# Scatter DMAs of a graph layer on GpSimd: a wait on TensorE's work two blocks on is taken out

## The chip, the cores and the metric

The kernel runs on one core of one Trainium2 chip. The metric is the device time of one launch in microseconds (us), from the start to the end of the program on that core; lower is better. PE is TensorE, DVE is VectorE, ACT is ScalarE, POOL is GpSimd and SP is SyncE. A "DMA" here is a transfer that one of these engines issues and that the core's 16 DMA engines carry out.

## The reference

One message-passing layer on a graph with 6250 nodes of 64 features and 206250 edges of 64 features, followed by a residual and a layer norm:

```python
row, col = edge_index                      # src, dst
msg = concat([x[col], edge_attr], axis=1)  # 206250 x 128
h = relu(msg @ W1a.T + b1a)
h = h @ W1b.T + b1b
agg = segment_sum(h, row, 6250) / maximum(counts, 1)[:, None]
z = relu(concat([x, agg], axis=1) @ W2a.T + b2a) @ W2b.T + b2b
out = concat([z, x], axis=1) @ Wr.T + br
return layernorm(x + out)
```

The work is in `relu(msg @ W1a.T + b1a)` for every edge and in the sum of these rows over the edges of a node. The edges come sorted by `dst`, so a run of edges needs few different rows of `x` for `col`; their `src` is in no order, so the rows have to be brought together by node before they are summed.

## The kernel before, in words

**Blocks.** The edges are cut into 124 blocks of 13 tiles of 128 edges. For each block the kernel computes the first layer's rows (`relu(...)`, 128 numbers, a count of 1 and the low bits of the node, 130 floats in all) into one of four SBUF buffers `orow0` to `orow3`, block k into buffer k % 4, and writes them to slots in DRAM that are grouped by node (128 nodes to a bin, 49 bins). Later, groups of slots are read back (`read`, L1457, tile `rt`) and summed by node: DVE builds a 0/1 matrix of slot against node (L1486, tile `oh`), PE multiplies it with the rows (L1505), and DVE adds the result to `part` (L1565).

**Two kinds of row.** In blocks 4 to 103 some of the edges are "joined": PE first sums up to four edges of the same node (L1267 and L1280, with the matrix `marks` of L1235, L1240 and L1241), and one row of the sum is kept, in a row of four that is called a quad. A block has two such joins of 3 tiles each, and nine of the blocks (9, 11, ... 25) have three. So a block has 13 tiles of single rows outside blocks 4 to 103, 7 with two joins, and 4 with three; to these come 2 or 3 joins.

**Scatters.** Each tile of single rows, and each join, is written to DRAM by one indirect DMA that POOL issues, with 128 slots that DVE has computed (`rowidx`, L1204, and `qidx`, L1167): L1395 for single rows and L1366 for quads. There are 985 of the one and 209 of the other, 1194 in all: 13 for a block with no join, 9 with two joins, 7 with three.

**Order.** PE, ACT, DVE and SP run in the order of the program text, which is written out by hand. Iteration k of the main loop has, in this order, the number of each edge's slot for block k + 1, the rows of block k, the sums that are due, and `scatter(k - LEAD)` with `LEAD = 2`. POOL's scatters are not in this fixed order: they are placed by the scheduler of the framework by when it reckons that their inputs are there. On the chip POOL then takes them strictly in the order that was placed, and one that waits holds up all behind it.

**Who waits for a scatter.** `low_bits(k)` (L1346, on ACT) is the first to write to block k's buffer, and waits until all scatters of block k - 4 have landed; the evictions from PSUM to the buffer follow it on ACT (L1358 for single rows, L1283 for quads). Reads (L1457, on SP) wait for the scatters whose rows they may hold, and the last group of reads for all of them. After the last scatter come only these last sums and the second layer of the nodes that are summed. The lines that matter:

```python
def low_bits(k):                                            # ACT, L1346
    ...
    nc.scalar.copy(orow_of(k, j0, BLK - j0)[:, :, H + 1], lo[:, k * BLK + j0 : (k + 1) * BLK])

def hidden(k, parts):                                       # PE L1355, ACT L1358
    ...
        done[k, c] = nc.tensor.matmul(ps[:, j, :], rhs[:WIDE, ...], m[:WIDE, :H], ...).ins.name
    nc.scalar.activation(orow_of(k, k0, n)[:, :, :H], ps[:, :n, :], AF.Relu)

def join_rows(k, i):                                        # PE L1280, ACT L1283
    ...
    done[k, f"join{i}"] = nc.tensor.matmul(ps[:, j, :], rj[:, ...], m, ...).ins.name
    nc.scalar.activation(mrow[:, g0 : g0 + 2, :], ps, AF.Relu)
```

The dictionary `done` keeps the names of PE's instructions: the matmul of tile c of block k, the last of its i-th join, and the last matmul of the first sum of iteration k (`"first"`) and of its rest (`"rest"`, both L1505).

Of the kernel before, what the change touches and what calls it, by code (L numbers as in the profile page):

```python
# [469 lines left out]
LEAD = 2  # L470
JOIN, QUAD, MARKS = 3, 4, 3
# [15 lines left out]
def fast_path(  # L487
# [42 lines left out]
    NGR = NT // NG  # L530
# [3 lines left out]
    BLK = NG  # L534
# [17 lines left out]
    def joined(k):  # L552
        if not JOIN_FROM <= k < JOIN_TO:
            return 0
        return 3 if k in THRICE else 2
# [194 lines left out]
    with (  # L750
# [16 lines left out]
        def orow_of(k, j, n=1):  # L767

            c = ROOM - BLK + j
            return orows[k % ROWS][:, c : c + n, :]  # L770

        def mrow_of(k, i):
            return orows[k % ROWS][:, i * QUAD : (i + 1) * QUAD, :]
# [252 lines left out]
        def bins_of(k):  # L1026


            ep_ = epoch_of[k]
            c0, j0 = k * BLK, JOIN * joined(k)  # L1030
            oh = ohs.pop(k)
            if joined(k) != joined(k - 1):
                starts_at(joined(k))
            t = direct(k) + 1
            had = slp.tile([P, 2 * HALF * t], BF16, name="had", padded_shape=[P, 2 * HALF * T])
            by_bin = oh.rearrange("p (b t) -> p b t", t=t)
            if j0:
                g = joined(k)
                joh = johs[k] = slp.tile([P, JOIN, g, NQB], BF16, name="joh", padded_shape=[P, JOIN, JOINS, NQB])
                nc.vector.tensor_tensor(  # L1040
                    joh,
                    ramp[:, None, None, :NQB].to_broadcast([P, JOIN, g, NQB]),
                    hi[:, c0 : c0 + j0].rearrange("p (j t) -> p t j", t=JOIN)[:, :, :, None].to_broadcast([P, JOIN, g, NQB]),
                    op=ALU.is_equal,
                )
            nc.vector.tensor_tensor(
                by_bin[:, :, 1:],
                ramp[:, : 2 * HALF, None].to_broadcast([P, 2 * HALF, BLK - j0]),
                hi[:, None, c0 + j0 : c0 + BLK].to_broadcast([P, 2 * HALF, BLK - j0]),
                op=ALU.is_equal,  # L1050
            )
            nc.vector.tensor_tensor_scan(had, on[:, : 2 * HALF * t], oh, 0.0, op0=ALU.mult, op1=ALU.add)  # L1052
            oh, had = (v.rearrange("p (b t) -> p b t", t=t) for v in (oh, had))
            hads[k] = had
            return oh, had
# [282 lines left out]
        done = {}  # L1338
# [21 lines left out]
        def scatter(k):  # L1360
            ep_ = epoch_of[k]
            e = epochs.index(ep_)
            j0 = JOIN * joined(k)
            for i in range(joined(k)):
                q = join_at[k] + i
                s = nc.gpsimd.indirect_dma_start(  # L1366
                    out=qep.rows.rearrange("(q r) f -> q (r f)", r=QUAD),
                    out_offset=bass.IndirectOffsetOnAxis(ap=qidx[:, q : q + 1], axis=0),
                    in_=mrow_of(k, i).rearrange("p r f -> p (r f)"),
                    in_offset=None,  # L1370
                )
                tc.declare_no_dep(s.ins, group="qslots", reason="each slot is written once")
                tc.add_to_no_dep_group("qslots", s.ins)
                tc.add_to_no_dep_group(f"qblock{k}", s.ins)
                scattered["q", k, i] = s.ins.name
                if k < EARLY:
                    tc.declare_no_dep(s.ins, group="qcleared", reason="no edge has these slots yet")
                if k == EARLY and i == 0:
                    for c in qcleared:
                        tc.add_manual_dep(  # L1380
                            s.ins, c.name,
                            mybir.DependencyInfo(mybir.DependencyClass.Sync, mybir.DependencyReason.DATA),
                            reason="edges may have these slots",
                        )
                for j, st in enumerate(qep.steps[:-1]):
                    if st.at <= k:
                        tc.declare_no_dep(s.ins, group=f"qreads{j}", reason="later edges have later slots")
            pace = (
                {9: BLK - 1, 10: "join0", 11: "join1", 12: "join2"} if j0 == 3 * JOIN
                else {6: 9, 8: BLK - 1, 10: "join0", 12: "join1"} if j0 == 2 * JOIN  # L1390
                else {j0: 9, j0 + 2: "first", 7: BLK - 1, 9: "join0", 11: "rest"}
            )
            for j in range(j0, BLK):
                t = k * BLK + j
                s = nc.gpsimd.indirect_dma_start(  # L1395
                    out=ep_.rows,
                    out_offset=bass.IndirectOffsetOnAxis(
                        ap=rowidx[:, k % RING * BLK + j : k % RING * BLK + j + 1], axis=0
                    ),
                    in_=orow_of(k, j)[:, 0, :],  # L1400
                    in_offset=None,
                )
                tc.declare_no_dep(s.ins, group=f"slots{e}", reason="each slot is written once")
                tc.add_to_no_dep_group(f"slots{e}", s.ins)
                tc.add_to_no_dep_group(f"block{k}", s.ins)
                scattered[t] = s.ins.name
                later = (min(k + LEAD, NGR - 1), pace.get(j))
                if later in done:
                    tc.add_manual_dep(
                        s.ins, done[later],  # L1410
                        mybir.DependencyInfo(mybir.DependencyClass.Sync, mybir.DependencyReason.DATA),
                        reason="first-layer rows are kept ahead of the scatters",
                    )
                for i, st in enumerate(ep_.steps[:-1]):
                    if st.at <= k:
                        tc.declare_no_dep(s.ins, group=f"reads{i}", reason="later edges have later slots")
                if k < EARLY:
                    tc.declare_no_dep(s.ins, group="cleared", reason="no edge has these slots yet")
                if k == EARLY and j == 0:
                    for c in cleared:  # L1420
                        tc.add_manual_dep(
                            s.ins, c.name,
                            mybir.DependencyInfo(mybir.DependencyClass.Sync, mybir.DependencyReason.DATA),
                            reason="edges may have these slots",
                        )
# [261 lines left out]
        for k, ep_ in enumerate(epoch_of):  # L1687
# [7 lines left out]
            j0 = JOIN * joined(k)  # L1695
# [7 lines left out]
            if k == 0:  # L1703
# [5 lines left out]
                ahead = bins_of(1)  # L1709
# [30 lines left out]
            if k + 2 < NGR:  # L1740
                columns(k + 2)
                ahead = bins_of(k + 2)
# [74 lines left out]
            if k >= LEAD:  # L1817
                scatter(k - LEAD)
# [15 lines left out]
        for k in range(NGR - LEAD, NGR):  # L1834
            scatter(k)
# [188 lines left out]
```

## Time and profile before

| | |
|---|---|
| three runs, median (lowest to highest) | 1638.09 us (1637.46 to 1638.39) |
| the profiled execution's own time | 1640.12 us |
| its span, first to last instruction | 1638.2 us |
| PE, DVE, ACT, POOL busy | 88%, 83%, 67%, 71% of the span |
| mean granted clock of PE | 0.96 |
| DMA | 393.44 MB, 240 GB/s over the span |

The profiled execution is 0.12% above the median of the three runs, and 1.9 us of its time lie outside the span. In the rows of the profile, `x985` is a count of instructions, the two numbers behind it are their busy time in us and the mean of one in ns, and what stands behind the second bar is the idle time of the engine just before them with what ended it. "issue" means that the engine waited for nothing that the profile shows. In a timeline a row has the start in us, the duration in us, the engine, the line and the operation, and in brackets the idle time before it and its releaser.

### The profile page before, as it was taken

What the parts mean: (1) busy time and instruction counts of PE and PEld (TensorE: products, weight loads), DVE (VectorE), ACT (ScalarE), POOL (GpSimd) and SP (SyncE); (2) the same over time, 40 slices, a digit from 0 to 9 for tenths busy, and PEclk for the clock granted to TensorE, in tenths of its full rate; (3) what the DMA queues carried; (4) which work ended last, traced back from release to release, by engine and by line L of the source; (5) the groups of instructions that cost most, each with busy time, mean ns of one, the idle gap of its engine ahead of it and who ended that gap; (6) DMA issues with size and microseconds to landing.
All of it is one profiled execution on the core that took longest, in us unless ns stands there. A gap on an engine that the chain in (4) does not pass through costs nothing.

```text
span 1638.2 us, 33212 instructions
## 1 busy us (share of the span) xinstructions
PE 1436.9 (88%) x10881; PEld 1306.3 (80%) x10881; DVE 1359.4 (83%) x3176; ACT 1102.8 (67%) x2247; POOL 1160.3 (71%) x1250
## 2 busy tenths in 40 slices
PE   6688888989999999999999999999986998799587
PEld 5577777778888888888888888888876998798476
DVE  7598888887888888999999999999966886776476
ACT  3289999987877777778878788877852344332044
POOL 6777777777777777777777777777776777777700
PEclk9699999999999999999999999999988999999788
DMA  8768888887887988677677667676879999897472
GB/s 208 218 227 288 289 285 293 293 262 240 251 259 227 269 237 246 203 231 216 202 222 217 216 204 235 199 227 194 237 229 342 324 324 290 265 280 241 132 207 78
DMA packets 230179, 393.44 MB, mean 240 GB/s; under 512 B 43205, under 2 KB 164935, under 8 KB 229743
## 3 DMA queue, kind: packets, MB, share of 16 engines
q1 hardware_dynamic: 155629, 224.57, 48.4%
q0 software_dynamic: 48240, 121.28, 21.0%
q10 hardware_dynamic: 26130, 45.38, 7.9%
q8 instruction: 89, 1.46, 0.4%
q14 instruction: 91, 0.75, 0.1%
HBM read 217.82 MB, written 173.25 MB: 239 GB/s over the span
## 4 chain that ended last, share of the span: by engine, by line
PE 55%; ACT 15%; DMA 14%; DVE 8%; issue 4%; POOL 2%; ACTq 1%; SPq 0%; DVEq 0%; POOLq 0%
PE h_ps L1505 23%; PE h_ps L1267 11%; DMA rows<-orow,rowidx 9%; PE h_ps L1355 9%; PE h_ps L1280 5%; ACT rhs L1320 4%; ACT rj L1272 3%; ACT orow L1283 2%; POOL rows L1395 2%; DMA rt<-rows 2%; DVE marks L1235 1%; ACT orow L1358 1%; ACT marks L1240 1%; ACT rhs L1318 1%; PE cnt_ps L1094 1%
## 5 line engine op out<-in xcount | busy, mean ns | idle before, releaser
L1395 POOL DMA_INDIRECT rows<-orow,rowidx x985 | 952.6, 967 | 329.8 <-issue 174.1
L1505 PE MATMUL h_ps<-rt,oh 128*128 128x129 f32 x4036 | 504.0, 280 | 43.8 <-DVE oh L1486 39.4
L1505 PEld LDWEIGHTS h_ps<-rt,oh 128*128 128x128 f32 x4036 | 479.3, 195 | 46.5 <-issue 40.8
L1486 DVE TENSOR_TENSOR oh<-ramp,rt 128x768 f32<-128x768 bf16 (+2 forms) x427 | 317.8, 779 | 46.0 <-DMA rt<-rows 42.3
L1267 PE MATMUL h_ps<-marks,side 128*128 128x512 f32 x1254 | 317.3, 402 | 2.8 <-ACT xr_now L1655 2.2
L1355 PE MATMUL h_ps<-mv,rhs 124*128 124x128 f32 x1970 | 278.3, 287 | 31.6 <-ACT orow L1358 31.5
L1280 PE MATMUL h_ps<-mv,rj 128*128 128x130 f32 x1672 | 234.1, 286 | 72.4 <-ACT orow L1283 45.5
L1280 PEld LDWEIGHTS h_ps<-mv,rj 128*128 128x128 f32 x1672 | 212.8, 193 | 106.2 <-ACT orow L1283 57.6
L1355 PEld LDWEIGHTS h_ps<-mv,rhs 124*128 124x128 f32 x1970 | 249.6, 198 | 35.8 <-ACT orow L1358 33.4
L1267 PEld LDWEIGHTS h_ps<-marks,side 128*128 128x128 f32 x1254 | 229.7, 190 | 48.3 <-ACT xr_now L1655 3.5
L1235 DVE TENSOR_TENSOR marks<-quad_ramp,ramp 128x1024 fp32r<-128x1024 f32 x209 | 250.6, 1203 | 0.0
L1366 POOL DMA_INDIRECT quads<-orow,qidx x209 | 202.3, 968 | 66.1 <-issue 18.4
L1358 ACT ACTIVATE orow<-h_ps 128x384 f32<-128x384 f32 (+1 forms) x287 | 151.4, 536 | 143.5 <-PE h_ps L1355 138.0
L1272 ACT COPY rj<-h_ps 128x512 f32<-128x512 f32 x209 | 119.7, 588 | 77.4 <-PE h_ps L1267 76.8
L1565 DVE TENSOR_TENSOR part<-part,h_ps 128x387 f32<-128x387 f32 (+2 forms) x232 | 113.1, 488 | 68.4 <-PE h_ps L1505 67.6
L1241 ACT ACTIVATE marks<-marks,ones 128x512 fp32r<-128x512 f32 x209 | 150.9, 722 | 6.8
L1283 ACT ACTIVATE orow<-h_ps 128x260 f32<-128x260 f32 x418 | 139.8, 389 | 23.3 <-PE h_ps L1280 19.4
L1240 ACT ACTIVATE marks<-quad_ramp,z_act 128x512 fp32r<-128x512 f32 x209 | 149.4, 715 | 0.0
L1052 DVE TENSOR_TENSOR_SCAN had<-ramp,bins 128x400 bf16<-128x400 bf16 (+1 forms) x124 | 135.0, 1089 | 17.1 <-ACT bins L1073 4.5
L1318 ACT ACTIVATE rhs<-rhs,from_win 60x896 f32<-60x896 bf16 (+1 forms) x116 | 130.5, 1125 | 2.9
L1320 ACT ACTIVATE rhs<-rhs,ones 60x896 f32<-60x896 f32 (+1 forms) x116 | 130.2, 1122 | 2.9
L1346 ACT CAST orow<-lo 128x7 f32<-128x7 bf16 (+1 forms) x124 | 24.2, 195 | 150.9 <-DMA rows<-orow,rowidx 139.1
(189 smaller groups left out, 1471.9 us busy)
## 6 DMA issues: line engine op xcount, KB each, us to landing
rt<-rows SPq DMA_DIRECT2D x145, 390.0 KB
rt<-quads SPq DMA_DIRECT2D x98, 390.0 KB
rhs<-in_edgeT SPq DMA_DIRECT2D x91, 224.0 KB
rt<-rows SPq DMA_DIRECT2D x98, 195.0 KB
enat<-in_edgeJ SPq DMA_DIRECT2D x91, 192.0 KB
rows<-orow,rowidx POOLq DMA_INDIRECT x985
rows<-padrow ACTq DMA_DIRECT2D x12, 1300.0 KB
quads<-padrow ACTq DMA_DIRECT2D x11, 1300.0 KB
```

Source lines behind the costliest of these rows:

```text
L1235: nc.vector.tensor_tensor(m[:, :n, :], all_q[:, None, :].to_broadcast([P, n, QUAD * P]), z[:, :n, None].to_broadcast([P, n, QUAD * P]), op ...
L1267: nc.tensor.matmul(ps, s[:, p, i * JOIN + t, :], m[:, t, :], start=t + p == 0, stop=t == JOIN - 1 and p == 1,)
L1272: nc.scalar.copy(rj, ps)
L1280: done[k, f"join{i}"] = nc.tensor.matmul(ps[:, j, :], rj[:, (g0 + j) * P : (g0 + j + 1) * P], m, start=True, stop=True).ins.name
L1283: nc.scalar.activation(mrow[:, g0 : g0 + 2, :], ps, AF.Relu)
L1320: nc.scalar.activation(rhs[D:WIDE, :], rhs[D:WIDE, :], AF.Relu, bias=ones[D:WIDE, :1], scale=-1.0)
L1355: done[k, c] = nc.tensor.matmul(ps[:, j, :], rhs[:WIDE, of * P : (of + 1) * P], m[:WIDE, :H], start=True, stop=True).ins.name
L1358: nc.scalar.activation(orow_of(k, k0, n)[:, :, :H], ps[:, :n, :], AF.Relu)
L1366: s = nc.gpsimd.indirect_dma_start(out=qep.rows.rearrange("(q r) f -> q (r f)", r=QUAD), out_offset=bass.IndirectOffsetOnAxis(ap=qidx[:, q ...
L1395: s = nc.gpsimd.indirect_dma_start(out=ep_.rows, out_offset=bass.IndirectOffsetOnAxis(ap=rowidx[:, k % RING * BLK + j : k % RING * BLK + j ...
L1486: nc.vector.tensor_tensor(res[:, at_tile : at_tile + nb * n, :], ramp[:, None, :].to_broadcast([P, nb * n, P]), node[:, :, None].to_broadc ...
L1505: m = nc.tensor.matmul(of_bin(b), oh[:, at_tile, :], rt[:, j * n + t, : H + 1], start=t0 + t == st.lo[b], stop=t0 + t == st.hi[b] - 1,)
```

## The change

In `scatter(k)`, the table `pace` and the dependency made from it are taken out. The table gave some of the single-row scatters of block k one more thing to wait for: a given piece of PE's work on block k + 2, such as the matmul of tile 9 or tile 12 or the last matmul of a join. Without it a scatter waits for its rows (ACT), for its slot numbers (DVE), and for the scatter eight places ahead of it to have landed, as all scatters did before and do now.

```diff
             def scatter(k):
                 ...
-            pace = (
-                {9: BLK - 1, 10: "join0", 11: "join1", 12: "join2"} if j0 == 3 * JOIN
-                else {6: 9, 8: BLK - 1, 10: "join0", 12: "join1"} if j0 == 2 * JOIN
-                else {j0: 9, j0 + 2: "first", 7: BLK - 1, 9: "join0", 11: "rest"}
-            )
             for j in range(j0, BLK):
                 t = k * BLK + j
                 s = nc.gpsimd.indirect_dma_start(
                 ...
                 scattered[t] = s.ins.name
-                later = (min(k + LEAD, NGR - 1), pace.get(j))
-                if later in done:
-                    tc.add_manual_dep(
-                        s.ins, done[later],
-                        mybir.DependencyInfo(mybir.DependencyClass.Sync, mybir.DependencyReason.DATA),
-                        reason="first-layer rows are kept ahead of the scatters",
-                    )
```

The instructions of PE, DVE, ACT and SP keep their order. On POOL the number and the kind of the instructions stay as they are, and their order changes. The first place is POOL where block 59 begins (buffers: 56 in `orow0`, 57 in `orow1`, 58 in `orow2`, 59 in `orow3`). In brackets stands what a scatter waits for: a DMASW number is the scatter eight places ahead of it. Before:

```order
L1366 DMA quads_66<-orow2_141,qidx_222 54976x520 [waits DMASW6_49,DVE_49,Activation_49]
L1395 DMA rows0_64<-orow0_139,rowidx_103 125440x130 [waits DMASW7_49,PE_49]
L1366 DMA quads_66<-orow2_141,qidx_222 54976x520 [waits DMASW0_49,Activation_49]
L1395 DMA rows0_64<-orow1_140,rowidx_103 125440x130 [waits DMASW1_49,PE_49]
L1395 DMA rows0_64<-orow3_142,rowidx_103 125440x130 [waits DMASW2_49,DVE_49,Activation_49]
L1395 DMA rows0_64<-orow3_142,rowidx_103 125440x130 [waits DMASW3_49]
L1395 DMA rows0_64<-orow1_140,rowidx_103 125440x130 [waits DMASW4_49,PE_49]
L1395 DMA rows0_64<-orow3_142,rowidx_103 125440x130 [waits DMASW5_49,Activation_49]
L1395 DMA rows0_64<-orow1_140,rowidx_103 125440x130 [waits DMASW6_49,PE_49]
```

The fifth row is block 59's first scatter. Ahead of it stand 522 scatters; three of block 57's and four of block 58's, all with a wait on PE, come after it, between those of blocks 59 and 60. The same place now:

```order
L1390 DMA rows0_64<-orow2_141,rowidx_103 125440x130 [waits DMASW6_49]
L1366 DMA quads_66<-orow2_141,qidx_222 54976x520 [waits DMASW7_49,DVE_49,Activation_49]
L1366 DMA quads_66<-orow2_141,qidx_222 54976x520 [waits DMASW0_49,Activation_49]
L1390 DMA rows0_64<-orow3_142,rowidx_103 125440x130 [waits DMASW1_49,DVE_49,Activation_49]
L1390 DMA rows0_64<-orow3_142,rowidx_103 125440x130 [waits DMASW2_49]
L1390 DMA rows0_64<-orow3_142,rowidx_103 125440x130 [waits DMASW3_49]
```

Each block's scatters stand together, in the order of the blocks: 529 of them, all of blocks 0 to 58, are ahead of block 59's first, and none waits for PE. L1390 is the former L1395; the change takes out lines above it.

The second place is POOL where block 107 begins (13 tiles to a block, no joins; 104 is in `orow0`, 105 in `orow1`, 106 in `orow2`, 107 in `orow3`). Before:

```order
L1395 DMA rows0_64<-orow0_139,rowidx_103 125440x130 x3
L1395 DMA rows0_64<-orow2_141,rowidx_103 125440x130 x5
L1395 DMA rows0_64<-orow3_142,rowidx_103 125440x130 x2
L1395 DMA rows0_64<-orow1_140,rowidx_103 125440x130
L1395 DMA rows0_64<-orow3_142,rowidx_103 125440x130 x2
L1395 DMA rows0_64<-orow1_140,rowidx_103 125440x130 x3
L1395 DMA rows0_64<-orow3_142,rowidx_103 125440x130 x6
```

And now:

```order
L1366 DMA quads_66<-orow3_142,qidx_222 54976x520 x2
L1390 DMA rows0_64<-orow0_139,rowidx_103 125440x130 x13
L1390 DMA rows0_64<-orow1_140,rowidx_103 125440x130 x13
L1390 DMA rows0_64<-orow2_141,rowidx_103 125440x130 x13
L1390 DMA rows0_64<-orow3_142,rowidx_103 125440x130 x13
```

Before, four tiles of block 105 and four of block 106 are left over when block 107 begins (the third row of before); now none is.

## The prediction

> **What bounds the kernel now.** I read the page's busy times first, then the idle time ahead of POOL's scatters, then the timelines. By busy time POOL looks idle for three tenths of the span.
>
> ```profile
> PE 1436.9 (88%) x10881; PEld 1306.3 (80%) x10881; DVE 1359.4 (83%) x3176; ACT 1102.8 (67%) x2247; POOL 1160.3 (71%) x1250
> L1395 POOL DMA_INDIRECT rows<-orow,rowidx x985 | 952.6, 967 | 329.8 <-issue 174.1
> L1366 POOL DMA_INDIRECT quads<-orow,qidx x209 | 202.3, 968 | 66.1 <-issue 18.4
> ```
>
> The waits, grouped (us in total, times, longest):
>
> ```profile
> POOL rows L1395 <- issue: 174.1, 571, 0.3
> ACT orow L1346 <- DMA rows<-orow,rowidx: 139.1, 23, 13.7
> ```
>
> 571 of POOL's gaps end without any wait, and each is 174.1 / 571 = 0.305 us. So a scatter costs POOL 0.967 + 0.305 = 1.272 us even when nothing holds it. 1194 of them take 1193 x 0.305 + 952.6 + 202.3 = 1518.8 us.
>
> ```profile
> 14.15 1.13 POOL L1395 DMA_INDIRECT rows<-orow,rowidx  x1 [8.04 <-ACT orow L1358]
> 1555.99 0.95 POOL L1395 DMA_INDIRECT rows<-orow,rowidx  x1 [0.30 <-issue]
> ```
>
> The first scatter starts at 14.15 and the last ends at 1556.94, 1542.8 us later. POOL is therefore held up for only 1542.8 - 1518.8 = 24.0 us in the whole run (the same from the groups: 329.8 + 66.1 - 8.04 ahead of the first - 363.9 = 24.0). From 14 to 1557 us POOL is the limit or close to it. Other engines stand ahead of it: ACT's 139.1 us is `low_bits` waiting for scatters of four blocks earlier to free a buffer. The stages (busy us and count by engine, granted clock, DMA share, GB/s):
>
> ```profile
> 340.00:699.20 359.20, 331.82 (x2518) 299.94 (x2516) 308.01 (x745) 284.04 (x571) 265.21 (x276) 1.00 0.80 241
> 1267.80:1380.00 112.20, 112.20 (x995) 110.77 (x994) 98.12 (x175) 46.47 (x62) 85.03 (x89) 1.00 1.02 320
> 1557.00:1638.20 81.20, 63.38 (x477) 57.36 (x477) 57.50 (x160) 38.74 (x182) 0.00 (x0) 0.88 0.50 143
> ```
>
> Between 340 and 699 PE is busy for 92%, and POOL issues 276 scatters, which at 1.272 us would take 351 of the 359 us: here PE's chain sets the pace, POOL waits a little. After the last scatter there are 81.3 us of last sums. PE's view of that seam:
>
> ```profile
> 1562.99 6.22 PE L1505 MATMUL h_ps<-rt,oh 128*128 128x129 f32 x36 [26.68 <-DVE oh L1486]
> ```
>
> PE has nothing to do for 26.68 us and then starts 6 us after the last scatter's end. So the end of the run is the end of POOL's scatters plus 81.3 us.
>
> **The change, part by part.** *Removed:* the wait on PE. What it costs is seen where a scatter with that wait has a gap over 0.3 us, as in these two:
>
> ```profile
> 651.97 0.96 POOL L1395 DMA_INDIRECT rows<-orow,rowidx  x1 [1.11 <-PE h_ps L1355]
> 658.96 0.95 POOL L1395 DMA_INDIRECT rows<-orow,rowidx  x1 [0.97 <-PE h_ps L1280]
> 626.48 0.60 ACT L1358 ACTIVATE orow<-h_ps 128x512 f32<-128x512 f32 x1
> 630.04 0.49 ACT L1358 ACTIVATE orow<-h_ps 128x384 f32<-128x384 f32 x1
> ```
>
> By the order these scatters are tiles 9 and 11 of block 53; ACT's two rows are the evictions that made their rows, 25 and 28 us earlier. They wait for block 55's PE work, and lose 1.11 - 0.305 = 0.8 and 0.7 us of POOL. All such losses lie within the 24.0 us. That is the ceiling of any gain on POOL, unless a scatter itself gets cheaper.
>
> *Moved:* each block's three or four held-back scatters go two blocks earlier, to their own block. The gain is how far POOL is ahead at the last moment when it must wait for rows. I take block 59's first rows, near the end of the stretch that PE paces:
>
> ```profile
> 698.62 0.60 ACT L1358 ACTIVATE orow<-h_ps 128x512 f32<-128x512 f32 x1 [1.95 <-PE h_ps L1355]
> 0.00:699.20 699.20, 391.78 (x402) 0.96 0.81 253
> 0.00:699.20 699.20, 114.93 (x119) 0.96 0.81 253
> 0.00:699.20 699.20, 11.37 (x60) 0.96 0.81 253
> ```
>
> The last three rows are the counts up to 699.2 us of L1395, of L1366 and of ACT's L1346. The 60th `low_bits` is block 59's, and its rows are there at 698.62 + 0.60 = 699.22. By then POOL had issued 402 + 119 = 521. In the new order all of blocks 0 to 58 can be out: 529. Can POOL have done them? 14.15 + 529 x 1.272 = 687.0, 12 us before the rows of block 59 come, so yes, if the earlier rows come when they came before; POOL then waits out these 12 us in small gaps. That they do I take from PE, DVE and ACT having the same instructions in the same order, and waiting for no scatter yet at that time: in the timeline ACT's first waits for a buffer are these two:
>
> ```profile
> 329.93 0.20 ACT L1346 CAST orow<-lo 128x7 f32<-128x7 bf16 x1 [1.10 <-DMA quads<-orow,qidx]
> 1034.77 0.20 ACT L1346 CAST orow<-lo 128x7 f32<-128x7 bf16 x1 [4.00 <-DMA rows<-orow,rowidx]
> ```
>
> Eight scatters ahead are 8 x 1.272 = **10.2 us**. From there POOL has 665 left instead of 673.
>
> *Second term:* one long wait of POOL lies after 699, and it is for rows, not for PE's later work:
>
> ```profile
> 1268.12 0.96 POOL L1395 DMA_INDIRECT rows<-orow,rowidx  x1 [4.58 <-ACT orow L1358]
> 1258.72 1.42 DVE L1486 TENSOR_TENSOR oh<-ramp,rt 128x768 f32<-128x768 bf16 x2 [14.73 <-DMA rt<-rows]
> 1209.64 0.22 ACT L1346 CAST orow<-lo 128x13 f32<-128x13 bf16 x1 [7.25 <-DMA rows<-orow,rowidx]
> 1221.24 0.21 ACT L1346 CAST orow<-lo 128x13 f32<-128x13 bf16 x1 [5.78 <-DMA quads<-orow,qidx]
> 1210.39 1.65 PE L1355 MATMUL h_ps<-mv,rhs 124*128 124x128 f32 x6 [3.90 <-ACT orow L1358]
> 1221.99 1.35 PE L1355 MATMUL h_ps<-mv,rhs 124*128 124x128 f32 x6 [2.70 <-ACT orow L1358]
> ```
>
> At 1268.12 block 107's rows are late by 4.58 - 0.305 = 4.3 us, because DVE and then PE waited 14.73 us for reads. Just before, PE lost 3.90 + 2.70 = 6.6 us to buffers that scatters still held. With POOL 10 us ahead, and a buffer's last scatters no longer put off by two blocks, these 6.6 us go, and the rows come that much earlier, more than the 4.3 us that are needed. I take the whole **4.3 us**. The other end is none of it: if the rows come when they came, POOL stands there again, now with 973 scatters behind it where it had 965, and the gain stays at 8 x 1.272 = 10.2 us.
>
> *Added:* nothing on POOL; a scatter whose rows are late stops those behind it, but these are of later blocks, and ACT writes the rows in that order too. On SP the reads wait for the same scatters, which land earlier. The last sums keep their 81.3 us: PE's 26.68 us idle covers a gain of 14.5 us with 12 to spare, and would cover the whole 24.
>
> The sum: 10.2 + 4.3 = 14.5 us off POOL's end. On the profiled execution 1640.1 - 14.5 = 1625.6; that execution is 2.0 us above the median of the runs, 1638.1, so the forecast is **1624** us.
>
> *The bound on a dearer scatter.* Nothing here says that a scatter has to cost the same in a new place. The bounds are the trace's own: the shortest, the median and the longest, and one of the long ones beside what DVE does then.
>
> ```profile
> L1395 POOL DMA_INDIRECT rows<-orow,rowidx x985: 952/958/1780, 14.1 to 1556.0; - x197
> 249.40 0.75 DVE L1256 TENSOR_TENSOR side<-enat,side 128x576 fp32r<-128x576 f32 x1
> 249.51 1.47 POOL L1395 DMA_INDIRECT rows<-orow,rowidx  x1 [0.30 <-ACT rhs L1318]
> ```
>
> A scatter that meets DVE's L1256 (two operands in SBUF) took 1.47 instead of 0.96 us. The mean is only 967 - 958 = 9 ns over the median, so few meet it: all the stretching is worth 1194 x 0.009 = 11 us. I take it as unchanged, since POOL is as busy as before and falls on DVE's work as it comes; if it all went, 11 us less, and the other end is the slow rival below. The Trainium skill ("SBUF — State Buffer", section "Who interferes with whom") says that a DVE instruction with two SBUF inputs contends with a GpSimd instruction that reads SBUF, and that the loser blocks for the whole instruction; the pair of rows above agrees in kind. By that rule, struck in every block, the sum would be the dear rival's below, 1652; by the rows' mean it stays 1624.
>
> **The rivals.**
>
> *Rows late at 1268 all the same (chance 0.15).* If the 14.73 us wait for reads is set by the DMA engines (share 1.02 just after it), not by when PE came there, block 107's rows come at the old time, and the gain is the 10.2 us of the first term: 1638.1 - 10.2 = 1628. For it: that share. Against: the reads are issued from SP, which waits for PE to free their tiles.
>
> *POOL never held up (0.08).* If rows in the first 700 us also come faster, up to the whole 24.0 us goes: 1614. Against it speaks that POOL needs 687 us for what PE and ACT deliver in 699.
>
> *No lead (0.07).* The wait on PE is only exchanged for the wait on rows, and POOL is not ahead at block 59: 1638. Against it stands that rows in those two timeline pieces had been there for 25 us.
>
> *Dearer scatters (0.15), the other side.* When POOL waits for rows at each block's head, its scatters start at the same place in every block, and one of them could meet L1256 in every block. 100 blocks with joins at 1.47 - 0.96 = 0.51 us each are 51 us on POOL, 40 more than the 11 now. Blocks 4 to 58 would take 28 of the 51, some 23 more than now: the 12 us of slack there swallow half, the other 11 eat the lead of 10.2. Blocks 59 to 103 add 45 x 0.51 = 23, less their 6 of the 11: 17. The 4.3 us wait at 1268 goes, as POOL comes later. Together 1 + 17 - 4 = 14 us slower: 1652. It decides from a mean of some 990 ns on (12 + 14.5 us over 1194 scatters are 22 ns more than 967). What stays under that falls into the range.
>
> **How the numbers follow.** Chances: 0.55 for 1624, 0.15 for 1628, 0.08 for 1614, 0.07 for 1638, 0.15 for 1652. A measurement of this kernel can tell about 0.2%, 3.3 us, from no change. Faster: 0.55 + 0.15 + 0.08 = 0.78; same 0.07; slower 0.15. The range goes from 1614, the ceiling, up to 1640, which takes in all cases but most of the slow rival.
>
> **What would show it.** Right: the gaps of L1390 released by PE are at 0.3 us; POOL waits 10 to 17 us for rows before 700 us, at the first tile of a block, and for nothing afterwards; at block 59's first eviction 529 scatters are out; L1390 stays at 967 ns; ACT's wait at L1346 falls far below 139.1 us before 1300 us; the last scatter ends near 1542, and 81 us follow. Wrong: a mean of 980 ns or more for L1390 (dearer scatters), a wait of 10 us at block 107 (late rows), a tail longer than 81 us, or PE's blocks between 340 and 700 us taking longer than the 359.2 / 31 = 11.6 us that they take by L1346's count in this row:
>
> ```profile
> 340.00:699.20 359.20, 5.79 (x31) 1.00 0.80 241
> ```

## The result, and the profile after

| | before | after |
|---|---|---|
| first comparison, median (lowest to highest) | 1638.39 us (1637.46 to 1643.27, 5 runs) | 1623.01 us (1622.65 to 1631.46, 5 runs) |
| ratio (95% interval) | | 0.9903 (0.9882 to 0.9924) |
| second comparison, median | 1638.47 us (11 runs) | 1623.11 us (4 runs) |
| ratio (95% interval) | | 0.9902 (0.9887 to 0.9916) |

The ratios and their intervals, here and below, leave out runs in a slower state of the chip, so they need not be the quotient of two medians. The change takes 15.4 us off, where 14.5 were predicted. The profile that came with the first comparison is of an execution of 1631.46 us, 8 us above the median of its kernel, so the rows below are those of the second one (1624.47 us, span 1622.7); the first stands at the end of this section.

The page of the changed kernel, its busy times and POOL's two groups (busy us, mean ns | idle us ahead of them):

```profile
PE 1429.9 (88%) x10881; PEld 1302.1 (80%) x10881; DVE 1358.8 (84%) x3176; ACT 1105.3 (68%) x2247; POOL 1161.2 (72%) x1250
L1390 POOL DMA_INDIRECT rows<-orow,rowidx x985 | 952.4, 967 | 315.4 <-issue 217.3 <-ACT orow L1358 21.6 <-DMA rows<-orow,rowidx 14.6
L1366 POOL DMA_INDIRECT quads<-orow,qidx x209 | 203.4, 973 | 63.7 <-issue 20.1 <-ACT orow L1283 7.3 <-ACT rj L1272 6.4
```

A scatter costs what it cost, 967 ns and a gap of 217.3 / 713 = 0.305 us by the first row of the waits below. POOL's waits are the idle time less the time ahead of the first scatter and 1193 plain gaps: 315.4 + 63.7 - 8.0 - 363.9 = 7.2 us, where they were 24.0. No group of waits on PE is left on POOL.

The waits, grouped (us in total, times, longest):

```profile
POOL rows L1390 <- issue: 217.3, 713, 0.4
ACT orow L1346 <- DMA rows<-orow,rowidx: 27.0, 5, 10.6
```

ACT waits 27.0 us for buffers instead of 139.1. POOL's first and last scatter in the timeline, then the windows from 340 us to block 59's first scatter and of the tail:

```profile
14.17 1.13 POOL L1390 DMA_INDIRECT rows<-orow,rowidx  x1 [8.04 <-ACT orow L1358]
1540.14 0.96 POOL L1390 DMA_INDIRECT rows<-orow,rowidx  x1 [0.30 <-issue]
```

```profile
340.00:697.68 357.68, 330.72 (x2503) 299.14 (x2502) 306.70 (x743) 281.73 (x566) 266.59 (x276) 0.99 0.77 241
1541.10:1622.70 81.60, 64.16 (x477) 58.30 (x477) 57.64 (x160) 38.82 (x182) 0.01 (x1) 0.88 0.49 143
```

The last scatter ends at 1541.10 instead of 1556.94, 15.84 us sooner, and 81.60 us follow, where 81.3 did. The whole gain is in POOL's row of scatters. In the window from 340 us PE is busy for 92% of the time and POOL issues 276 scatters, both as before.

**Block 59.** ACT's eviction of its first rows, POOL's first scatter of them, and what POOL (L1390, L1366) and ACT (L1346) had issued up to then:

```profile
696.81 0.60 ACT L1358 ACTIVATE orow<-h_ps 128x512 f32<-128x512 f32 x1 [1.94 <-PE h_ps L1355]
697.68 0.96 POOL L1390 DMA_INDIRECT rows<-orow,rowidx  x1 [0.90 <-ACT orow L1358]
```

```profile
0.00:697.60 697.60, 398.43 (x410) 0.96 0.80 254
0.00:697.60 697.60, 116.31 (x119) 0.96 0.80 254
0.00:697.60 697.60, 11.37 (x60) 0.96 0.80 254
```

410 + 119 = 529 scatters are out when block 59's rows come, all of blocks 0 to 58. POOL waits 0.90 - 0.305 = 0.6 us for them, and that is its last wait. So 697.68 is the start of the 530th scatter. In the profile before, the 530th is this one:

```profile
709.92 0.96 POOL L1366 DMA_INDIRECT quads<-orow,qidx  x1 [0.30 <-DVE marks L1235]
```

Here POOL is 709.92 - 697.68 = 12.2 us ahead.

**Block 107.** The 974th scatter is its first. The long wait of DVE for reads, the eviction and the scatter, and then the eviction of the same rows in the profile before:

```profile
1246.12 1.42 DVE L1474 TENSOR_TENSOR oh<-ramp,rt 128x768 f32<-128x768 bf16 x2 [14.81 <-DMA rt<-rows]
1255.64 1.16 ACT L1358 ACTIVATE orow<-h_ps 128x512 f32<-128x512 f32 x2 [26.14 <-PE h_ps L1355]
1261.82 0.96 POOL L1390 DMA_INDIRECT rows<-orow,rowidx  x1 [0.30 <-DMA rows<-orow,rowidx]
```

```profile
1267.25 1.16 ACT L1358 ACTIVATE orow<-h_ps 128x512 f32<-128x512 f32 x2 [20.09 <-PE h_ps L1355]
```

DVE's wait for reads is as long as before (14.81 against 14.73 us), but it ends 12.6 us sooner, and the rows are there more than 5 us before POOL comes (the first of the two evictions ends at 1255.64 + 0.60 = 1256.24). The wait of 4.3 us is gone.

**The first profile** (execution of 1631.46 us) has longer waits of POOL in one place:

```profile
648.72 0.96 POOL L1390 DMA_INDIRECT rows<-orow,rowidx  x1 [3.57 <-DVE oh L1474]
658.77 0.96 POOL L1390 DMA_INDIRECT rows<-orow,rowidx  x1 [3.01 <-ACT orow L1358]
L1390 POOL DMA_INDIRECT rows<-orow,rowidx x985 | 952.0, 967 | 323.9 <-issue 210.7
```

In the second profile the same stretch has one wait, of 1.9 us at 650.76. In the first its waits sum to 17 us, and its scatters end at 1548.6. A stray delay there goes to the end like any other wait.

### The profile page after: what moved, and what is told of

Same layout as the page of the kernel before. It is cut to its first block, busy times and chain, and to the rows that moved or that the text cites. A ratio compares the mean times of both kernels' runs of the same rounds, so it can differ in the third digit from the quotient of the medians.

```text
span 1629.7 us, 33233 instructions
## 1 busy us (share of the span) xinstructions
PE 1433.4 (88%) x10881; PEld 1304.9 (80%) x10881; DVE 1358.3 (83%) x3176; ACT 1104.8 (68%) x2247; POOL 1159.2 (71%) x1250
## 4 chain that ended last, share of the span: by engine, by line
PE 54%; ACT 13%; DMA 11%; DVE 9%; issue 8%; POOL 5%; SPq 0%; ACTq 0%; DVEq 0%; POOLq 0%
PE h_ps L1493 21%; PE h_ps L1267 11%; PE h_ps L1355 9%; DMA rows<-orow,rowidx 7%; PE h_ps L1280 5%; POOL rows L1390 4%; ACT rj L1272 3%; DMA rt<-rows 2%; ACT orow L1283 2%; DVE marks L1235 2%; ACT rhs L1320 1%; ACT marks L1240 1%; ACT rhs L1318 1%; ACT orow L1358 1%; PE cnt_ps L1094 1%
## 5 line engine op out<-in xcount | busy, mean ns | idle before, releaser
L1390 POOL DMA_INDIRECT rows<-orow,rowidx x985 | 952.0, 967 | 323.9 <-issue 210.7
L1366 POOL DMA_INDIRECT quads<-orow,qidx x209 | 201.8, 966 | 64.7 <-issue 22.9
L1283 ACT ACTIVATE orow<-h_ps 128x260 f32<-128x260 f32 x418 | 139.4, 388 | 22.3 <-PE h_ps L1280 18.7
L1108 DVE TENSOR_SCALAR of_quads<-cnt_ps 128x98 bf16<-128x98 f32 x100 | 26.5, 265 | 79.5 <-PE cnt_ps L1098 78.1
```

The lines of the kernel that those rows point to most:

```text
L1366: s = nc.gpsimd.indirect_dma_start(out=qep.rows.rearrange("(q r) f -> q (r f)", r=QUAD), out_offset=bass.IndirectOffsetOnAxis(ap=qidx[:, q ...
L1390: s = nc.gpsimd.indirect_dma_start(out=ep_.rows, out_offset=bass.IndirectOffsetOnAxis(ap=rowidx[:, k % RING * BLK + j : k % RING * BLK + j ...
```

## The experiments

Three theories were put to the test. *Lead*: up to block 59 the rows set the pace, behind it POOL's scatters alone, and what counts is how many are out by then, and the row wait at block 107. *Wait*: each wait on PE costs its 0.75 us wherever it stands (in the profile before, 22 of the scatters that wait on PE are held up, for 16.4 us in all). *Buffer*: the gain comes from ACT's shorter waits for buffers. The first pair of expectations names two more: *Count*, by which every scatter costs its 1.272 us wherever it stands, and *PE*, by which PE's chain is the limit at every place.

### Ten scatters more, early or late

The last tile of a block is issued a second time, to a DRAM tensor that nothing reads, in blocks 28 to 37 or in blocks 62 to 71:

```diff
+        def scatter_again(k):
+            s = nc.gpsimd.indirect_dma_start(
+                out=spare_rows, out_offset=...(ap=rowidx[:, <tile 12 of block k>]),
+                in_=orow_of(k, BLK - 1)[:, 0, :], in_offset=None)
...
+                if 28 <= k - LEAD < 38:        # the late one: 62 <= k - LEAD < 72
+                    scatter_again(k - LEAD)
```

> The changed kernel with one more scatter at the end of each of blocks 28 to 37: POOL issues the block's last tile a second time, to a DRAM tensor that nothing reads. Ten more scatters, all before 700 us; nothing else is changed. Where the kernel before takes about 1638 us and the changed one about 1623: Lead theory (up to block 59 the rows set the pace and POOL has some 12 to 17 us of waits to give; after it POOL's scatters alone set the end): the ten take 10 x 1.272 = 12.7 us out of POOL's waits, and the end moves by 0 to 2 us: 1623 to 1625. Count theory (POOL is the limit from its first scatter to its last, and every scatter counts wherever it is): 1623 + 12.7 = 1636. If PE's chain is the limit at every place, 1623.

> The same ten more scatters, at the end of blocks 62 to 71 (about 730 to 850 us). Where the kernel before takes about 1638 us and the changed one about 1623: Lead theory: no wait is left there to take them up, so the whole 12.7 us go to the end: 1635 to 1637, which is the kernel before again. Count theory: 1636 as well, but then the early ten cost the same. If PE's chain is the limit and POOL follows it, 1623 to 1625, like the early ten. The two kernels differ in nothing but the blocks, so their difference is 11 to 13 us by the Lead theory and 0 by both others.

Measured, with 1638.24 us for the kernel before: early 1628.29 us (ratio 0.994, 0.9926 to 0.9953), late 1636.7 us (0.9986, 0.9975 to 0.9998). The late ten cost 13.6 us over the 1623.1 of the changed kernel, the early ten 5.2. POOL's group of single rows in the early one; then this group and the longest wait in the late one:

```profile
L1391 POOL DMA_INDIRECT rows<-orow,rowidx x985 | 949.3, 964 | 310.6 <-issue 215.8 <-DMA rows<-orow,rowidx 19.7 <-ACT orow L1359 16.8
```

```profile
L1391 POOL DMA_INDIRECT rows<-orow,rowidx x985 | 951.3, 966 | 318.6 <-issue 212.7 <-ACT orow L1359 26.3 <-DMA rows<-orow,rowidx 20.4
651.08 0.95 POOL L1391 DMA_INDIRECT rows<-orow,rowidx  x1 [2.23 <-ACT orow L1359]
```

The order of the cost is what Lead says, and Count and PE, which see no difference between the two, are refuted. The difference is 8.4 us, though, and not 11 to 13, for the size of the early ten was wrong: 12 to 17 us of waits were assumed to be there for the taking, as in the first profile. By the gaps in the timelines, the late one's waits come to about 10.4 us and the early one's to 2.5, so the ten filled 8 of their 12.7, and 4.7 were left for the end. They show at block 59, whose first scatter in the early one comes without a wait, 4.8 us after the 697.68 of the changed kernel:

```profile
702.47 0.96 POOL L1391 DMA_INDIRECT rows<-orow,rowidx  x1 [0.30 <-issue]
```

### The waits on PE in part of the blocks

```diff
-                if later in done:
+                if later in done and k < 57:      # early;   late: and k >= 100
```

> The kernel before, but with the wait on PE only in blocks 0 to 56. All scatters of blocks 0 to 58 stand ahead of block 59's first (529), and those of blocks 0 to 106 ahead of block 107's (973), as in the changed kernel; more than half of the waits on PE stay. Where the kernel before takes about 1638 us and the changed one 1623: Lead theory (what counts is how many scatters are out when PE's rows stop setting the pace, and the row wait at block 107): 1623 to 1626. Wait theory (each held-back scatter costs its 0.75 us of waiting, 16.5 us in all, nearly all of them before block 57): about 1636.

> The kernel before, but with the wait on PE only from block 100 on. 529 scatters stand ahead of block 59's first, as in the changed kernel, but 965 ahead of block 107's, as in the kernel before. Where the kernel before takes about 1638 us and the changed one 1623: Lead theory: the first term, 10 us, is there; at block 107 POOL comes 10 us earlier and stands before rows that are not there, so that part of it is lost again unless the rows come earlier as well: 1625 to 1634, with a wait of 3 us or more at block 107. Wait theory: hardly any waits are left, 1623. If the rows of block 107 come with POOL, 1627 (the 4.3 us stay lost).

> The changed kernel itself once more, beside the variants below and with a profile of its own. Where the kernel before takes about 1638 us, 1623 us; POOL's waits behind its first scatter sum to about 10 us and lie before 706 us, as in the run with ten scatters added late (10.6 us there), and its last scatter ends near 1541 us.

Early waits alone: 1632.01 us (ratio 0.9959, 0.9946 to 0.9972). Late waits alone: 1627.77 us (0.9933, 0.992 to 0.9946). The changed kernel beside them: 1623.11 us.

The early one misses the bounds of both theories. Counted as above, 15.6 us of waits on PE are still in it, nearly all that there were, and yet it gains 6.4 us, so Wait falls. Its POOL group, and three of its last waits:

```profile
L1395 POOL DMA_INDIRECT rows<-orow,rowidx x985 | 954.4, 969 | 323.3 <-issue 195.0 <-DMA rows<-orow,rowidx 15.2 <-PE h_ps L1280 13.3
652.32 0.96 POOL L1395 DMA_INDIRECT rows<-orow,rowidx  x1 [1.12 <-PE h_ps L1355]
659.27 0.96 POOL L1395 DMA_INDIRECT rows<-orow,rowidx  x1 [0.94 <-PE h_ps L1280]
660.75 0.96 POOL L1366 DMA_INDIRECT quads<-orow,qidx  x1 [0.52 <-ACT orow L1283]
```

The order would let 529 scatters go ahead of block 59, but the waits on PE, up to 661 us, do not let POOL get through them: the row at 660.75 is the 492nd, and 38 x 1.272 us later, at 709, POOL comes to block 59, 11 us after its first scatter of the changed kernel. So Lead in the form "count what stands ahead in the order" falls as well. What is left of it: POOL's last wait, wherever it is and whatever it is for, fixes the end; behind it every scatter costs 1.272 us.

The late one: the two first scatters of blocks 59 and 107 in its timeline, ACT's eviction at the latter, and its buffer waits:

```profile
698.02 0.96 POOL L1395 DMA_INDIRECT rows<-orow,rowidx  x1 [0.93 <-ACT orow L1358]
1253.17 0.96 POOL L1395 DMA_INDIRECT rows<-orow,rowidx  x1 [1.58 <-ACT orow L1358]
1252.30 1.16 ACT L1358 ACTIVATE orow<-h_ps 128x512 f32<-128x512 f32 x2 [18.13 <-PE h_ps L1355]
```

```profile
ACT orow L1346 <- DMA rows<-orow,rowidx: 121.3, 16, 13.8
```

With the old order from block 100 on, block 107's first is the 966th scatter again, and POOL waits there again, but for 1.3 us and not for 4.3: the rows come some 15 us earlier than before, with POOL 12 us ahead. The time lies in the range that Lead gave; its wait of 3 us or more at block 107 is not there. Wait, which gave 1623, misses. ACT has 121.3 us of buffer waits here, nearly what it had before, and 10.7 of the 15.4 us are gained all the same, so Buffer falls as the account of the gain. The profiled execution is as short (span 1623.0) as the changed kernel's, but it is the fastest of five. The median, 4.7 us above the changed kernel, is more than the 1.3 us of wait explain; one profile does not show the rest, and a share of ACT's waits in it is not ruled out.

### Held back by order alone, without a wait on PE

The changed kernel with an order for POOL written by hand. Order edges carry no wait. The table holds back four tiles of a block, but only part of its order edges are in the built program. In the order that results, two single-row tiles of most blocks, 9 and 12 (four in the kernel before), go two blocks later: one just ahead of that block's scatters and one between its two quads. 526 scatters stand ahead of block 59's first, and none waits on PE.

```diff
+PLACED = (0, 1, 2, ..., 1980)                 # block * 16 + tile, in POOL's order
...
+            prev: add_manual_dep(s.ins, <the scatter ahead>, NoSync)
```

> The changed kernel with its scatters put into an order by hand, no wait on PE: in each block two tiles are held back by two blocks, as in the kernel before four are. 526 scatters stand ahead of block 59's first (521 before, 529 in the changed kernel), 973 ahead of block 107's. Where the kernel before takes about 1638 us and the changed one 1623: Lead theory: three of the eight scatters of the lead are missing, 3 x 1.272 = 3.8 us, so 1625 to 1628. Wait theory: no wait on PE is there, so 1623.

Measured: 1632.45 us (0.9964, 0.995 to 0.9977), 9.3 us above the changed kernel, not 3.8. Two rows of its timeline, its first scatter of block 59, and the group of the quads (L1347 is L1283 of before, L1441 is L1366, L1468 is L1395):

```profile
199.37 0.96 POOL L1441 DMA_INDIRECT quads<-orow,qidx  x1 [2.83 <-ACT orow L1347]
590.64 0.96 POOL L1441 DMA_INDIRECT quads<-orow,qidx  x1 [1.65 <-ACT orow L1347]
702.91 0.96 POOL L1468 DMA_INDIRECT rows<-orow,rowidx  x1 [0.30 <-ACT side L1313]
L1441 POOL DMA_INDIRECT quads<-orow,qidx x209 | 202.3, 968 | 79.8 <-ACT orow L1347 26.5 <-issue 18.6 <-ACT rj L1336 6.1
```

Scatters whose rows have been ready for two blocks stand behind a quad that is not made yet, and POOL waits at its head: 308.6 us of idle time ahead of the single rows and 79.8 ahead of the quads give 308.6 + 79.8 - 8.0 - 363.9 = 16.5 us of waits. By these waits POOL comes to block 59 at 702.91, 5.2 us later than the changed kernel, and the three scatters that are missing from the lead cost 3.8 us more: 9.0 of the 9.3. No wait on PE is in this kernel, so Wait, which gave 1623, falls here too; what costs is any scatter at the head of the queue that is not ready while others behind it are.

### The account of all of them

| kernel | scatters | POOL's waits, us | last scatter ends | us behind it | median, us |
|---|---|---|---|---|---|
| before | 1194 | 24.0 | 1556.9 | 81.3 | 1638.4 |
| early waits | 1194 | 18.0 | 1552.3 | 81.4 | 1632.0 |
| held back by order | 1194 | 16.5 | 1549.0 | 81.4 | 1632.5 |
| late waits | 1194 | 11.0 | 1542.0 | 81.0 | 1627.8 |
| after | 1194 | 7.2 | 1541.1 | 81.6 | 1623.1 |
| ten more, late | 1204 | 10.4 | 1553.7 | 81.1 | 1636.7 |
| ten more, early | 1204 | 2.5 | 1544.7 | 80.6 | 1628.3 |

POOL's waits are the idle time ahead of its scatters, less 0.305 us for each. Scatters times 1.272 us, plus waits, plus the 14.2 us ahead and 81 behind, give the span of each profiled execution to 4 us or better (the early ten are the worst, since their scatters took 964 ns and not 967). As the waits are what the plain gaps leave over, this is an account and no test; what it shows is that a scatter's cost (965 to 969 ns and the gap of 0.305 us) and the 81 us (80.6 to 81.6) are nearly the same in all seven. The profiled execution of the early waits is 3.5 us above its median, that of the late waits 3.0 below.

### The same kernels on two other chips

The experiments above ran on the chips that the record numbers 3 and 13. On two others, 10 and 8, every kernel takes far longer: the one before 2119.39 and 2120.28 us. On chip 10 four of the kernels above ran as well, and on chip 8 two versions with fewer scatters, which take three joins instead of two in 5 or 9 more blocks between 61 and 93:

```diff
-THRICE = tuple(range(9, 27, 2))
+THRICE = (*range(9, 27, 2), *range(61, 97, 4))      # nine more; five: range(61, 101, 8)
```

> The changed kernel itself, for a profile beside those of the experiments and a second interval. All theories: 1623 us, as in the four runs that agree. The first profiled execution of it took 1631.5 us and has waits of 3.3 and 2.7 us at blocks 54 and 55; if these are a chance event, this profile has 10 to 14 us of POOL waiting for rows before 700 us, none of these two, and a last scatter that ends near 1540 us.

> The wait on TensorE is put back for blocks 0 to 56 alone. Lead theory (the gain is the eight scatters that POOL is ahead when block 59's rows come, and 4.3 us at block 107): the lead is gone and only the 4.3 us are left, 1634 us. Buffer theory (the gain is ScalarE's wait for buffers, nearly all of it after 1030 us): blocks from 57 on have the new order, so 1623 us. Wait theory (the gain is each wait on TensorE, wherever it stands; nearly all of them stand before 700 us): 1638 us.

> The wait on TensorE is put back for blocks 100 to 123 alone, so that at block 107 eight scatters are held back again. Lead theory: POOL comes to block 107 ten us earlier than before, but stands there until its rows come, and these come earlier only by what ScalarE no longer waited for buffers: 1628 us, between 1624 and 1632. Buffer theory: the late buffers are as before, 1636 to 1638 us. Wait theory: no wait on TensorE after block 100 cost anything, so 1623 us.

> No scatter waits for TensorE, but POOL's order holds two tiles of each block back by two blocks, so that 526 scatters stand ahead of block 59's first where the changed kernel has 529 and the kernel before 522. Lead theory: the order alone takes 3 of 8 scatters of the lead, 1623 + 3 x 1.27 = 1627 us, up to 1629 with the quads that wait a little more. Wait theory: no wait on TensorE, so 1623 us. Buffer theory: buffers come free about two blocks later than in the changed kernel, 1630 to 1638 us.

> The changed kernel with three joins instead of two in five more blocks (61, 69, 77, 85, 93): each takes three single-row scatters away and adds one quad, 10 scatters fewer in all, in the stretch where POOL sets the pace. In exchange PE has one more join in each of these blocks (6 matmuls of 512 columns and 8 of 130, some 2.6 us by the rows of the changed kernel between 706 and 1250 us, less 3 matmuls of L1355), DVE and ACT the matrix for it. Where the changed kernel takes 1623 us: Account theory (every us that POOL is spared behind block 59 comes off the end): 10 x 1.272 = 12.7 us off, 1610. PE theory (POOL then runs into rows that are not there): between 1610 and 1623, with new waits of POOL for rows after 700 us.

> The same in nine more blocks (every fourth from 61 to 93): 18 scatters fewer. Where the changed kernel takes 1623 us: Account theory: 18 x 1.272 = 22.9 us off, 1600. Between 706 and 1250 us PE is idle for 46 us of 544 and DVE for 54, and nine joins take some 9 x 2.2 = 20 us of PE, so it should hold. PE theory: POOL catches up with the rows and waits for them again: 1605 to 1615, with the waits in the blocks with three joins or just behind them. PE's idle time before the last sums (26.7 us in the kernel before) is the other bound: where the scatters end more than that much earlier, the last sums no longer wait for them alone.

| kernel | median, us | ratio to before there (95% interval) |
|---|---|---|
| before, chips 10 and 8 | 2119.39 and 2120.28 | |
| after | 2261.75 | 1.0591 (1.0536 to 1.0646) |
| early waits | 2193.38 | 1.0351 (1.0305 to 1.0396) |
| held back by order | 2189.62 | 1.0314 (1.0271 to 1.0357) |
| late waits | 2256.01 | 1.064 (1.0588 to 1.0691) |
| 10 scatters fewer, chip 8 | 2266.01 | 1.0674 (1.0616 to 1.0731) |
| 18 scatters fewer, chip 8 | 2265.01 | 1.0705 (1.0653 to 1.0757) |

All expectations missed there, since their starting point, POOL as the limit, does not hold. The page and one group of waits of the changed kernel on chip 10:

```profile
PE 1699.6 (75%) x10881; PEld 1501.9 (66%) x10881; DVE 1364.4 (60%) x3176; ACT 1113.1 (49%) x2247; POOL 1161.0 (51%) x1250
L1390 POOL DMA_INDIRECT rows<-orow,rowidx x985 | 954.8, 969 | 746.1 <-ACT orow L1358 452.5
```

```profile
POOL quads L1366 <- ACT orow L1283: 230.5, 117, 4.8
```

A scatter takes the same 969 ns, but POOL now waits 452.5 + 230.5 us for rows, and 10 or 18 scatters fewer bring no gain: 2266 and 2265 us on chip 8, against 2262 for the changed kernel on chip 10, which was not measured on chip 8. How many blocks had begun (count of L1346) by 850 us, and between 850 and 1450, in the changed kernel:

```profile
0.00:850.00 850.00, 10.05 (x53) 0.84 0.59 188
850.00:1450.00 600.00, 6.91 (x37) 0.89 0.49 153
```

In the one with early waits, which has them up to block 56:

```profile
0.00:850.00 850.00, 10.80 (x57) 0.87 0.64 201
850.00:1450.00 600.00, 7.10 (x38) 0.89 0.50 154
```

57 blocks against 53 while its scatters are held back, and 38 against 37 when they no longer are. Held back everywhere (before) it is fastest, in half the blocks or with half the tiles in between. So on that chip the first layer, which comes ahead of the scatters, gets on faster while some of them are held back. Why is not settled. The clock granted to PE is lower (0.849 in the mean against 0.960), and it goes with the time: 0.871 to 0.883 in the runs of the kernel before there, 0.842 to 0.857 in those of the changed one; which of the two brings about the other is open. Engines wait for each other where no row of the profile names a late DMA, but the trace there holds only 17,461 semaphore updates (41,594 in the first profile of this kernel), so its releasers can't be trusted. No profile of the kernel before exists on these chips. Whether the versions with more joins beat 1623 us where POOL is the limit was not seen.

## Why the prediction was right, and where it was not

**POOL is the limit, and the tail is fixed.** Right: 81.6 us behind the last scatter, and the late ten scatters went to the end in full.

**The ceiling of 24.0 us and the cost of 1.272 us.** Right. L1390 stays at 967 ns; the rival of dearer scatters did not come. The Trainium skill ("SBUF — State Buffer", section "Who interferes with whom") says that a DVE instruction with two SBUF inputs contends with a GpSimd instruction that reads SBUF. The unchanged mean shows no more of that in the new order.

**The lead at block 59.** Right in place and count, 529 out and the last wait there. The term was a little small: at the 530th scatter POOL is 12.2 us ahead, not 10.2. Block 59's rows came at 697.41, 1.8 us sooner than the 699.22 that the prediction kept, and 10.2 + 1.8 = 12.0. That they would come as before was its assumption, and here it erred. The change need not be the reason: in the first profile of the same kernel they came at 705.38. With the 4.3 of block 107 the gain would be 16.5; some 0.6 of it go to scatters that took a little longer behind it, and 15.84 are left. How much of the 1.8 us is there in every execution stays open, so part of how near 14.5 came to 15.4 may be luck.

**Waits before 700 us.** It said 10 to 17 us, at first tiles of blocks. They are at first tiles, but sum to 7.2 us in the second profile; in the first they are 17, not all of them at first tiles.

**The row wait at block 107.** Right that all 4.3 us go. Its reason was a part of the matter: the rows came not 6.6 but 11.6 us sooner (first eviction over at 1256.24 against 1267.85). Before, ACT waited for buffers again and again from 1034 us on; with the change this is the first such wait in its timeline:

```profile
1398.94 0.22 ACT L1346 CAST orow<-lo 128x13 f32<-128x13 bf16 x1 [1.36 <-DMA rows<-orow,rowidx]
```

The rival of reads that come late all the same is refuted by DVE's wait, which moved 12.6 us forward with the chain.

**What counts as a lead.** The prediction read the lead from the order, with a proviso on POOL's time. The proviso is the real condition: with early waits kept, the order gives the same 529, and 8.9 us of the 15.4 are lost.

**A slip.** The two scatters at 651.97 and 658.96, called tiles 9 and 11 of block 53, are tiles 6 and 10 by the table of the change; their evictions are those quoted, so the argument stands.

## What to carry to other kernels

Where one in-order engine is the limit, add up its waits, instruction by instruction, and see where the last one stands: a wait ahead of that moment may cost nothing, one that becomes the last moves the end in full. A wait or an order that puts a transfer not yet ready ahead of ready ones costs that engine time even if every transfer comes early enough for its reader. And test such a change where the limit is another engine as well: here the same edit gains 1% on some chips and costs 6% on another.

## What the runs showed of the hardware that was not expected

The kernel before took 1638 us on chips 3 and 13 (26 runs that agree within 0.6%) and 2119 and 2120 us on chips 10 and 8 (22 runs within 1.5%), and on chip 10 the sign of this change is the other one. In the profile of the late waits, 121 us of ACT's buffer waits go with a span of 1623.0 us; in that of the changed kernel it is 27 us, with 1622.7.

A scatter's DMA packets end with 16 short ones of 4 bytes. Counted in order of time, these have ended 3.5 us after the scatter starts (median before and after; 7.5 at most). As one starts every 1.272 us, about three are under way at a time, and the scatter eight places ahead has always landed, at least 2.6 us early, so the wait for it holds none up. The gap of 0.305 us between scatters is the same in all eight profiles in which POOL is the limit (174.1 / 571 before, 217.3 / 713 after).
